# Graph attention in pairs of key tiles: three PSUM score tiles in one exponential, the scores issued in two fours, and the first head loads spread over the projection loop

## The chip, the cores and the metric

The kernel runs on one core of one Trainium2 chip. The metric is the device time of one execution in microseconds (us). A profiled execution gives a span (first to last instruction on the core) and a trace of every instruction. Engine names: PE is TensorE (matmuls), PEld its weight loads, ACT is ScalarE, DVE is VectorE, POOL is GpSimd, and SP is the engine whose queue issues most DMAs.

## The reference, cut to what matters

Four graph layers run one after the other on x (3327 nodes, 128 features) with an adjacency matrix adj of 0 and 1. The change lies in the second, an attention over all nodes with 128 heads of width 8 (n, m run over nodes, d over the 128 heads, h over the 8 elements of a head). Both biases of the score are adj, so 2·adj is added:

```python
q = (x @ Wq.T).reshape(d, n, h)
k = (x @ Wk.T).reshape(d, n, h)
v = (x @ Wv.T).reshape(d, n, h)
a = jnp.einsum('dnh,dmh->dnm', q, k) * scale
a = a + spatial_encoding + edge_encoding      # both are adj
a = jax.nn.softmax(a, axis=2)
out = jnp.einsum('dnm,dmh->dnh', a, v)
```

So there are 128 × 3327 × 3327 scores, and each needs a product, an addition of 2·adj, an exponential, and a weighted sum with v. The sum of the exponentials comes out of the same product as the weighted values, since v carries a ninth column of ones.

## The kernel before

The first layer fills the first 345 us of the profile, the preparation of the attention (projections, L422 to L498) runs to about 566, the attention itself (L500 to L628) from there to 10470, and the two last layers take the rest.

**Preparation.** A loop over 26 row tiles r projects q, k and v. ACT copies each product out of PSUM into a staging tile (`qk_st`, `v_st`; four buffers of each), and SP stores it to DRAM. A fresh `v_st` tile needs its column of ones, which POOL writes with a memset in each round (L473). From r = 2 on, one entry of the list `early` is emitted in each round: `Parting` loads queries and keys back, splits each into a rounded part and a rest, and stores both (L356 to L381); `load_heads(0, 0)` loads the keys, queries and values of the first four heads, 20 DMAs in one entry; `key_pair` rounds two key tiles on POOL (L419); `exp_of` makes exponentials of 2·adj (L347). Outside the hand-ordered part, a scheduler may move instructions of one engine past each other.

**Attention.** Queries are taken in 7 chunks of 476 columns (the last 471, run as 472), heads in 32 groups of four, keys in 26 tiles t of 128. So there are 7 × 32 × 26 = 5824 steps, or 2912 pairs of an even and an odd key tile. The order on every engine is that of the program text (`manual_schedule`, L578). Head i of a group lies on rows 32i to 32i + 31, so four score matmuls can run side by side on four row groups. `WAYS` (L505) says how 2·adj gets into a score: D, DVE adds it while it moves the scores out of PSUM (L552); I, an identity matmul adds it in PSUM (L550); G, POOL multiplies the finished exponential by exp(2·adj) (L555). An even tile is D, D, D, I and an odd one D, D, I, G. D scores go to the PSUM tile `early`, four buffers of one bank. I and G scores go to the tile `late`, one bank for an even tile and two for an odd one, one buffer each. A last bank, `acc`, takes the weighted sums. ACT exponentiates the `late` scores directly (L553, once per step), and the five D scores of a pair in one instruction in SBUF (L557). `weigh` (L559) issues the four value matmuls of the step four steps back; they use four column groups, in two passes each. At the end of a group, DVE copies `acc` out (L573).

On PE, a step is: four scores, identity product or products, weigh. On ACT, a pair is: exponential of 476 columns, of 952, of 2380.

Of the kernel before, what the change touches and what calls it, by code (L numbers as in the profile page):

```python
# [8 lines left out]
F32 = mybir.dt.float32  # L9
# [6 lines left out]
AF = mybir.ActivationFunctionType  # L16
# [5 lines left out]
P = 128  # L22
# [32 lines left out]
def kernel(  # L55
# [285 lines left out]
    def even(c):  # L341
        w = q_chunks[c][1]
        return w + w % 2
# [45 lines left out]
                if t == 11:  # L389
                    self.store(side)  # L390

    def load_heads(c, g):
        q0, w = q_chunks[c]
        k_in = kq.tile([P, NP], F32, name="k_in", bufs=1)
        q4 = kq.tile([P, QW], F32R, name="q4")
        v4 = kq.tile([P, 4, T, EA], F32, name="v4")
        nc.gpsimd.memset(k_in[:, N:], 0.0)
        if w % 2:
            nc.gpsimd.memset(q4[:, w : w + 1].bitcast(F32), 0.0)
        for i in range(4):  # L400
            n0 = (4 * g + i) * N
            for j in range(2):
                r = 32 * i + HL * j
                nc.sync.dma_start(k_in[r : r + HL, :N], kt[:, n0 : n0 + N])
                nc.sync.dma_start(q4[r : r + HL, :w].bitcast(F32), dram(qt, E * j * GP + n0 + q0, [[0, 2], [GP, E], [1, w]]))
        for i in range(4):
            n0 = (4 * g + i) * N
            nc.sync.dma_start(
                v4[:, i].rearrange("p t e -> p (t e)"),
                vd[n0 : n0 + NP, :].rearrange("(p t) e -> p (t e)", t=T),  # L410
            )
        return k_in, q4, v4, []

    def key_pair(heads):
# [7 lines left out]
    with tc.tile_pool(name="l1", bufs=1) as pool, tc.tile_pool(name="l1_ps", bufs=3, space=PSUM) as ps:  # L422
        w_st = pool.tile([D, 3, NH * E], F32, name="w_st")
        for i, w in enumerate((wq, wk, wv)):
            nc.gpsimd.dma_start(w_st[:, i, :], w)
        zero = pool.tile([HL, NH], F32, name="zero")
        nc.vector.memset(zero, 0.0)
        nc.gpsimd.dma_start(vd[N * NH : N * NH + 1, :], zero[:1, :EA])
        for end in (qf, kf):
            nc.gpsimd.dma_start(end[:E, N * NH :], zero[:E])  # L430

        with tc.tile_pool(name="l1_ln", bufs=1) as ln, tc.tile_pool(name="l1_tp", bufs=2, space=PSUM) as tps:
            h, done = layernorm_relu(ln)
            done(T)
            hT = transposed(pool, tps, h, "hT")
        st = ctx_st.enter_context(tc.tile_pool(name="l1_st", bufs=4))

        def store(dst, src, r, kp):
            for p0, p1 in ((0, kp),) if kp == P else ((0, 112), (112, kp)):
                nc.sync.dma_start(dst[r * P + p0 : r * P + p1], src[p0:p1])  # L440


        assert 7 * N + NP <= 2 * P * NH
        early = []
        for g in range(2):
            part = Parting(g)
            for side in range(2):
                early.append(lambda part=part: (part.load(0), part.load(1)) if part.lo[0] is None else None)
                early.append(lambda part=part, side=side: [part.part(side, i) for i in range(4)] and part.store(side))
        first, e_first = [], []  # L450
        early.append(lambda: first.extend(load_heads(0, 0)))
        ahead_part = Parting(2)
        early.append(lambda: (ahead_part.load(0), ahead_part.load(1)))
        early.append(lambda: e_first.extend(exp_of(a, 0) for a in a_first[1::2]))
        early += [lambda: (key_pair(first), key_pair(first))] * (T // 4)
        if T // 2 % 2:
            early.append(lambda: key_pair(first))
        for r in range(T):
            kp = rows_of(r)
            lhs = hT[:, r * P : r * P + kp]  # L460
            for i, (dst, mx) in enumerate(((qf, q_max), (kf, k_max))):
                pp = ps.tile([P, 2, 512], F32, name="pp", bufs=2)
                for c in range(2):
                    nc.tensor.matmul(pp[:kp, c, :], lhs, w_st[:, i, c * 512 : c * 512 + 512], start=True, stop=True)
                s = st.tile([P, E * NH], F32, name="qk_st")
                nc.scalar.activation(s[:kp], pp[:kp].rearrange("p a b -> p (a b)"), AF.Copy, scale=D**-0.5 if i == 0 else 1.0)
                nc.vector.tensor_reduce(mx[:kp, r : r + 1], s[:kp], AX.X, ALU.max, apply_absolute_value=True)
                store(dst[:E].rearrange("e (r c) -> r e c", c=NH), s.rearrange("p (e c) -> p e c", c=NH), r, kp)
            pp = ps.tile([P, 2, 512], F32, name="pp", bufs=2)
            for c in range(2):  # L470
                nc.tensor.matmul(pp[:kp, c, :], lhs, w_st[:, 2, c * 512 : c * 512 + 512], start=True, stop=True)
            s = st.tile([P, NH, EA], F32, name="v_st")
            nc.gpsimd.memset(s[:, :, E : E + 1], 1.0)  # L473
            nc.scalar.copy(s[:kp, :, :E], pp[:kp].rearrange("p a (c e) -> p (a c) e", e=E))
            store(vd.rearrange("(r c) e -> r (c e)", c=NH), s.rearrange("p c e -> p (c e)"), r, kp)

            if r > 1 and early:
                early.pop(0)()
        while early:
            early.pop(0)()  # L480

        mx4 = pool.tile([P, 4], F32, name="mx4")
        for i, m in enumerate((q_max, k_max, a_max, low_bits)):
            nc.vector.tensor_reduce(mx4[:, i : i + 1], m, AX.X, ALU.max)
        all4 = pool.tile([P, 4], F32, name="all4")
        nc.gpsimd.partition_all_reduce(all4, mx4, P, bass_isa.ReduceOp.max)
        bound = pool.tile([P, 1], F32, name="bound")
        nc.vector.tensor_mul(bound, all4[:, 0:1], all4[:, 1:2])  # L490
        nc.vector.tensor_scalar_mul(bound, bound, 1.01 * E / 2)
        nc.vector.tensor_add(bound, bound, all4[:, 2:3])
        fits = pool.tile([P, 2], F32, name="fits")
        nc.vector.tensor_scalar(fits[:, 0:1], bound, SAFE / 2, None, op0=ALU.is_le)
        nc.vector.tensor_scalar(fits[:, 1:2], all4[:, 3:4], 0.0, None, op0=ALU.is_equal)
        nc.vector.tensor_mul(unsafe, fits[:, 0:1], fits[:, 1:2])
        nc.vector.tensor_scalar(unsafe, unsafe, -1.0, 1.0, op0=ALU.mult, op1=ALU.add)
        ctx_st.close()  # L498
# [3 lines left out]

    WAYS = ("DDDI", "DDIG")  # L505
    PLACES = ((0, 1, 2, 5), (3, 4, 6, 7))
    two_i = const.tile([P, P], BF16, name="two_i")
    nc.vector.tensor_copy(two_i, ident)
    engines = {
# [9 lines left out]
    with tc.tile_pool(name="at_in", bufs=1) as a_pool, tc.tile_pool(name="at_p", bufs=3) as p_pool, tc.tile_pool(  # L519
# [13 lines left out]
            q0, w = q_chunks[c]  # L533
            nc.sync.dma_start(adj16[t][:, q0 : q0 + w], a2[:, :w])

        def scores(step, heads, a2, e_a, p8):
            c, _, t = step
            we = even(c)
            _, q4, _, pairs = heads
            ways, places = WAYS[t % 2], PLACES[t % 2]  # L540
            n_d = ways.count("D")
            late = ps.tile([P, 4 - n_d, 512], F32, name=f"late{4 - n_d}")
            early = [ps.tile([P, 512], F32, name="early", bufs=4) for _ in range(n_d)]
            for i in (*range(n_d, 4), *range(n_d)):
                r = slice(32 * i, 32 * i + 32)
                sp = early[i] if i < n_d else late[:, i - n_d]
                nc.tensor.matmul(sp[:, :we], pairs[t // 2][r, t % 2, :], q4[r, :we], start=True, stop=ways[i] != "I")  # L547
            for i in range(4):
                if ways[i] == "I":
                    nc.tensor.matmul(late[:, i - n_d, :we], two_i, a2[:, :we], start=False, stop=True)  # L550
            for i in range(n_d):
                nc.vector.tensor_tensor(p8[:, places[i], :we], early[i][:, :we], a2[:, :we], op=ALU.add)  # L552
            nc.scalar.activation(p8[:, places[n_d] : places[3] + 1, :we], late[:, :, :we], AF.Exp)  # L553
            if ways[3] == "G":
                nc.gpsimd.tensor_tensor(p8[:, places[3], :we], p8[:, places[3], :we], e_a[:, :we], op=ALU.mult)  # L555
            if t % 2:
                nc.scalar.activation(p8[:, :5, :we], p8[:, :5, :we], AF.Exp)  # L557

        def weigh(step, v4, p8):  # L559
            c, g, t = step  # L560
# [17 lines left out]
        with tc.manual_schedule(engines=engines):  # L578
# [7 lines left out]
            for j, step in enumerate(steps):  # L586
# [6 lines left out]
                        a_t, a_next = a_next, []  # L593
                        e_t, e_next = e_next, []
                if t % 2 == 0:
                    p8 = p_pool.tile([P, 8, QW], F32, name="p8")
                scores(step, heads, a_t[t], e_t[t // 2], p8)
                begun[j] = (step, heads[2], p8)
                if j >= ahead:
                    weigh(*begun.pop(j - ahead))  # L600
                if t == min(4, T // 2) and more:
                    coming = load_heads(*groups[n])
                if c == 0 and g + 2 < n_groups:
# [506 lines left out]
```

## Time and profile before

| | |
|---|---|
| median of 3 runs | 11194.51 us (11192.19 to 11195.0) |
| profiled execution, its time | 11195.14 us |
| profiled execution, its span | 11193.4 us |
| TensorE clock granted | 0.989 |
| attention stage in the trace | 566 to 10470 us |
| PE, ACT, DVE, POOL busy over the span | 97, 91, 83, 54% |

In a row of the groups view, the columns are: line, engine, operation, output from input, shapes, count, then busy time and mean ns of one, then the idle time of the engine just before these instructions and what ended it. In the timeline, each row has start, duration, engine, line and a count of merged instructions. An ACT instruction's duration holds the time that it waits behind the one before it, so durations of successive rows overlap; the steps between starts and between ends tell the rate. Durations of PE matmuls are modelled and overlap as well.

### The profile page before, as it was taken

The numbers are of one execution on the slowest core, as the hardware profiler recorded it, in microseconds if no ns is written. First come the engines' busy times: TensorE is split into PE (matmuls) and PEld (weight loads), VectorE is DVE, ScalarE is ACT, GpSimd is POOL, SyncE is SP. The second block draws the span as 40 slices with busy tenths as digits, with TensorE's granted clock in tenths as the row PEclk, the third lists the DMA queues.
The fourth block names the chain that finished last, engine by engine and source line by source line (L and its number), as shares of the span: only waits on it lengthen the run. The fifth ranks groups of instructions, "written<-read, shape, count | busy, mean of one in ns | idle before, by whom it ended". The sixth has DMA issues, their size and how long they took to land. (4 is left out here: it accounts for less than half of the span.)

```text
span 11193.4 us, 209350 instructions
## 1 busy us (share of the span) xinstructions
PE 10850.5 (97%) x79530; PEld 3005.9 (27%) x79530; DVE 9343.1 (83%) x15429; ACT 10199.3 (91%) x9152; POOL 6016.3 (54%) x6964
## 2 busy tenths in 40 slices
PE   9899999999999999999999999999999999999996
PEld 4322222222222222222222222222222222222453
DVE  8588888888888888888888888888888888888656
ACT  0399999999999999999999999999999999999522
POOL 0277777555555555555555555555555555555203
PEclk9899999999999999999999999999999999999998
DMA  7755554333333333333333333333333332333432
GB/s 264 238 129 120 123 127 109 65 64 64 68 64 62 67 66 63 68 65 61 68 66 63 66 66 61 67 66 61 66 66 61 66 63 55 61 58 58 135 113 97
DMA packets 417541, 942.25 MB, mean 84 GB/s; under 512 B 67936, under 2 KB 345937, under 8 KB 380940
## 3 DMA queue, kind: packets, MB, share of 16 engines
q1 hardware_dynamic: 412762, 918.98, 37.4%
q8 instruction: 627, 10.27, 0.4%
q0 software_dynamic: 3760, 9.78, 0.3%
q14 instruction: 392, 3.21, 0.1%
HBM read 788.78 MB, written 139.71 MB: 83 GB/s over the span
## 5 line engine op out<-in xcount | busy, mean ns | idle before, releaser
L552 DVE TENSOR_TENSOR p<-early,a 128x476 f32<-128x476 f32 (+1 forms) x14560 | 8426.4, 646 | 1369.4 <-PE early L547 1297.5
L557 ACT ACTIVATE p<-p 128x2380 f32<-128x2380 f32 (+1 forms) x2912 | 7568.4, 2599 | 0.4
L564 PE MATMUL acc<-p,v 128*9 128x476 f32 (+1 forms) x46592 | 5748.5, 564 | 15.3 <-ACT p L557 1.4
L553 ACT ACTIVATE p<-late 128x476 f32<-128x476 f32 (+1 forms) x5824 | 5315.4, 1175 | 13.8 <-DMA q<-qt 10.2
L555 POOL TENSOR_TENSOR p<-p,e 128x476 f32<-128x476 f32 (+1 forms) x2912 | 3528.1, 1212 | 3204.3 <-ACT p L553 2998.6
L547 PE MATMUL late<-q,k 32*128 32x476 f32 (+1 forms) x8736 | 2798.2, 478 | 99.5 <-ACT p L553 39.7
L547 PE MATMUL early<-q,k 32*128 32x476 f32 (+1 forms) x14560 | 2843.6, 478 | 9.4 <-DVE p L552 9.4
L419 POOL CAST k<-k_in 128x256 fp32r<-128x256 f32 x2912 | 1936.5, 697 | 886.4 <-DMA k_in<-kt 339.4
L547 PEld LDWEIGHTS late<-q,k 32*128 32x128 f32 x8736 | 1065.4, 181 | 4890.4 <-ACT p L553 4186.2
L550 PE MATMUL late<-a,two_i 128*128 128x476 bf16 (+1 forms) x5824 | 2180.8, 374 | 0.0
L547 PEld LDWEIGHTS early<-q,k 32*128 32x128 f32 x14560 | 1113.0, 181 | 9.9 <-DVE p L552 9.9
L564 PEld LDWEIGHTS acc<-p,v 128*9 128x9 f32 x46592 | 695.2, 88 | 1272.6 <-issue 1185.8
L550 PEld LDWEIGHTS <-two_i 128*128 128x128 bf16 x5824 | 556.2, 96 | 1329.0 <-issue 1329.0
L189 ACT COPY agg<-agg_ps 128x512 f32<-128x512 f32 x15 | 8.2, 591 | 485.5 <-PE agg_ps L204 290.6
L230 PE MATMUL agg_ps<-a,part 128*128 128x512 bf16 (+1 forms) x1092 | 227.0, 369 | 4.3 <-ACT agg L928 3.2
L272 POOL TENSOR_SCALAR a<-a_in 128x476 bf16<-128x476 f32 (+2 forms) x156 | 221.1, 1417 | 0.5
L272 POOL TENSOR_SCALAR a<-a 128x476 bf16<-128x476 f32 (+1 forms) x26 | 36.4, 1400 | 288.1 <-DMA a<-in_adjT_dram 288.1
L923 PE MATMUL sp<-yT,hT 128*128 128x512 f32 (+1 forms) x364 | 170.7, 610 | 12.3 <-ACT agg L928 6.4
L204 PE MATMUL agg_ps<-a,h 128*128 128x512 f32 (+2 forms) x364 | 148.2, 570 | 26.2 <-DVE h L164 26.2
L573 DVE COPY o<-acc 105x476 f32<-105x476 f32 (+1 forms) x224 | 144.5, 645 | 4.6 <-PE acc L564 4.6
L204 PE MATMUL agg_ps<-a,x 128*128 128x512 f32 (+2 forms) x364 | 145.3, 562 | 0.6 <-ACT x L318 0.6
L230 PEld LDWEIGHTS <-part 128*128 128x128 f16 x1092 | 108.6, 99 | 117.7 <-issue 10.3
(236 smaller groups left out, 2592.0 us busy)
## 6 DMA issues: line engine op xcount, KB each, us to landing
k_in<-kt SPq DMA_DIRECT2D x1792, 207.9 KB
v<-vd SPq DMA_DIRECT2D x896, 117.0 KB
a<-in_adjT_dram SPq DMA_DIRECT2D x50, 1663.5 KB
a<-adj SPq DMA_DIRECT2D x78, 831.8 KB
q<-qt SPq DMA_DIRECT2D x1536, 29.8 KB
a_in<-in_adjT_dram SPq DMA_DIRECT2D x125, 238.0 KB
adj<-a SPq DMA_DIRECT2D x156, 119.0 KB
vd<-v_st SPq DMA_DIRECT2D x25, 576.0 KB
```

The lines of the kernel that those rows point to most:

```text
L204: nc.tensor.matmul(acc[c][:, :w], lhs[:kp, t, :], a[:kp, c0 : c0 + w], start=(t == 0), stop=(t == T - 1))
L230: nc.tensor.matmul(acc[c][:, :w], part[:, t, :], a[:, c0 : c0 + w], start=(t == 0 and i == 0), stop=(t == T - 1 and i == len(parts) - 1),)
L272: nc.gpsimd.tensor_scalar(a2[:kp, :w], a, 2.0, None, op0=ALU.mult)
L419: nc.gpsimd.tensor_copy(k, slots(k_in)[:, t : t + 2, :])
L547: nc.tensor.matmul(sp[:, :we], pairs[t // 2][r, t % 2, :], q4[r, :we], start=True, stop=ways[i] != "I")
L550: nc.tensor.matmul(late[:, i - n_d, :we], two_i, a2[:, :we], start=False, stop=True)
L552: nc.vector.tensor_tensor(p8[:, places[i], :we], early[i][:, :we], a2[:, :we], op=ALU.add)
L553: nc.scalar.activation(p8[:, places[n_d] : places[3] + 1, :we], late[:, :, :we], AF.Exp)
L555: nc.gpsimd.tensor_tensor(p8[:, places[3], :we], p8[:, places[3], :we], e_a[:, :we], op=ALU.mult)
L557: nc.scalar.activation(p8[:, :5, :we], p8[:, :5, :we], AF.Exp)
L564: nc.tensor.matmul(acc[32 * i : 32 * i + EA, :w], v4[:kp, i, t, :], p8[:kp, PLACES[t % 2][i], :w], start=(t == 0), stop=(t == T - 1),)
L923: nc.tensor.matmul(sp[:, c0 : c0 + w], slots(zT)[:, t, :], z2T[:, cols], start=True, stop=False)
```

## The change

Four edits are made together.

1. `WAYS` of an even tile becomes I, D, D, D. `scores` is called once for a pair. The three `late` scores of a pair (the even tile's I, the odd tile's I and G) share one tile of three banks, in one buffer, and one exponential of 3 × 476 columns. `early` keeps its four banks, so all eight banks are in use as before.
2. The eight scores of a pair are issued as two fours, each on four row groups. The first four are all D (even heads 1, 2, 3 and odd head 0). The second are the three late ones and the fifth D (odd head 1). Between the two fours goes the weigh of the even tile; after the second come both identity products, one behind the other, and then the weigh of the odd tile.
3. POOL's multiplication is issued at the odd step (`times_e`), behind what POOL is given in the even step.
4. In the preparation, `load_heads(0, 0)` is cut in pieces: four entries with four key and query DMAs each, then one value DMA in each of the next four entries. Each of seven entries rounds two key tiles and makes two exponentials (the last entry has one of each). Two empty entries of `early` go. The four `v_st` tiles are made once, with the column of ones written before the loop.

The diff, cut to its core:

```diff
-    def load_heads(c, g):
+    def load_heads(c, g, pieces=None):
...
+        for f in (scored, weighted):
+            for i in range(4):
+                if pieces is None:
+                    f(i)
+                else:
+                    pieces.append(lambda f=f, i=i: f(i))
...
-        first, e_first = [], []
-        early.append(lambda: first.extend(load_heads(0, 0)))
         ahead_part = Parting(2)
         early.append(lambda: (ahead_part.load(0), ahead_part.load(1)))
-        early.append(lambda: e_first.extend(exp_of(a, 0) for a in a_first[1::2]))
-        early += [lambda: (key_pair(first), key_pair(first))] * (T // 4)
-        if T // 2 % 2:
-            early.append(lambda: key_pair(first))
+        pieces, e_first = [], []
+        first = load_heads(0, 0, pieces)
+        early += pieces[:4]
+        key_steps = -(-(T // 2) // 2)
+        for i in range(key_steps):
+            def step(i=i):
+                for f in pieces[4 + i : 5 + i if i < key_steps - 1 else None]:
+                    f()
+                for n in (2 * i, 2 * i + 1):
+                    if n < T // 2:
+                        key_pair(first)
+                        e_first.append(exp_of(a_first[2 * n + 1], 0))
+            early.append(step)
+        v_sts = [st.tile([P, NH, EA], F32, name=f"v_st{i}", bufs=1) for i in range(4)]
+        for s in v_sts:
+            nc.gpsimd.memset(s[:, :, E : E + 1], 1.0)
...
-            s = st.tile([P, NH, EA], F32, name="v_st")
-            nc.gpsimd.memset(s[:, :, E : E + 1], 1.0)
+            s = v_sts[r % 4]
...
-    WAYS = ("DDDI", "DDIG")
-    PLACES = ((0, 1, 2, 5), (3, 4, 6, 7))
+    WAYS = ("IDDD", "DDIG")
+    PLACES = ((5, 0, 1, 2), (3, 4, 6, 7))
+    FOURS = (((0, 1), (0, 2), (0, 3), (1, 0)), ((0, 0), (1, 2), (1, 3), (1, 1)))
...
+            p8 = p_pool.tile([P, 8, QW], F32, name="p8")
+            late = ps.tile([P, 3, 512], F32, name="late")
+            for n, four in enumerate(FOURS):
+                if n == 1:
+                    between()
+                for odd, i in four:
+                    way, place = WAYS[odd][i], PLACES[odd][i]
+                    sp = ps.tile([P, 512], F32, name="early", bufs=4) if way == "D" else late[:, place - 5]
+                    r = slice(32 * i, 32 * i + 32)
+                    nc.tensor.matmul(sp[:, :we], pairs[t // 2][r, odd, :], q4[r, :we], start=True, stop=way != "I")
+                    if way == "D":
+                        nc.vector.tensor_tensor(p8[:, place, :we], sp[:, :we], a2s[odd][:, :we], op=ALU.add)
+            for odd, i in FOURS[1]:
+                if WAYS[odd][i] == "I":
+                    nc.tensor.matmul(late[:, PLACES[odd][i] - 5, :we], two_i, a2s[odd][:, :we], start=False, stop=True)
+            nc.scalar.activation(p8[:, 5:, :we], late[:, :, :we], AF.Exp)
+            nc.scalar.activation(p8[:, :5, :we], p8[:, :5, :we], AF.Exp)
+            return p8
...
                 if t % 2 == 0:
-                    p8 = p_pool.tile([P, 8, QW], F32, name="p8")
-                scores(step, heads, a_t[t], e_t[t // 2], p8)
+                    p8 = scores(step, heads, a_t[t : t + 2], lambda: weigh(*begun.pop(j - ahead)) if j >= ahead else None)
+                else:
+                    times_e(step, p8, e_t[t // 2])
+                    if j >= ahead:
+                        weigh(*begun.pop(j - ahead))
                 begun[j] = (step, heads[2], p8)
-                if j >= ahead:
-                    weigh(*begun.pop(j - ahead))
```

More of the change, by code (lines that the diff above doesn't have):

```diff
@@ L399, in load_heads, with scored @@
             nc.gpsimd.memset(q4[:, w : w + 1].bitcast(F32), 0.0)
-        for i in range(4):
+        def scored(i):
             n0 = (4 * g + i) * N
@@ L405, in load_heads, with weighted @@
                 nc.sync.dma_start(q4[r : r + HL, :w].bitcast(F32), dram(qt, E * j * GP + n0 + q0, [[0, 2], [GP, E], [1, w]]))
-        for i in range(4):
+        def weighted(i):
             n0 = (4 * g + i) * N
@@ L447 @@
             for side in range(2):
-                early.append(lambda part=part: (part.load(0), part.load(1)) if part.lo[0] is None else None)
+                if side == 0:
+                    early.append(lambda part=part: (part.load(0), part.load(1)))
                 early.append(lambda part=part, side=side: [part.part(side, i) for i in range(4)] and part.store(side))
-        first, e_first = [], []
-        early.append(lambda: first.extend(load_heads(0, 0)))
         ahead_part = Parting(2)
         early.append(lambda: (ahead_part.load(0), ahead_part.load(1)))
-        early.append(lambda: e_first.extend(exp_of(a, 0) for a in a_first[1::2]))
-        early += [lambda: (key_pair(first), key_pair(first))] * (T // 4)
-        if T // 2 % 2:
-            early.append(lambda: key_pair(first))
+        pieces, e_first = [], []
[14 more added lines that the diff above has]
+            nc.gpsimd.memset(s[:, :, E : E + 1], 1.0)
         for r in range(T):
@@ L534, in store_adj, with scores @@
             nc.sync.dma_start(adj16[t][:, q0 : q0 + w], a2[:, :w])
-        def scores(step, heads, a2, e_a, p8):
+        def scores(step, heads, a2s, between):
             c, _, t = step
@@ L539, in scores @@
             _, q4, _, pairs = heads
[L540 to L555, printed above, removed]
@@ L556, in scores @@
-            if t % 2:
-                nc.scalar.activation(p8[:, :5, :we], p8[:, :5, :we], AF.Exp)
+            p8 = p_pool.tile([P, 8, QW], F32, name="p8")
[10 more added lines that the diff above has]
+                        nc.vector.tensor_tensor(p8[:, place, :we], sp[:, :we], a2s[odd][:, :we], op=ALU.add)
@@ new lines, in scores, with times_e @@
+            for odd, i in FOURS[1]:
[4 more added lines that the diff above has]
+            return p8
+        def times_e(step, p8, e_a):
+            we = even(step[0])
+            assert WAYS[1][3] == "G"
+            nc.gpsimd.tensor_tensor(p8[:, PLACES[1][3], :we], p8[:, PLACES[1][3], :we], e_a[:, :we], op=ALU.mult)
```

## The prediction

> **What bounds the kernel now.** I read the engine totals, then the busy time by stretches, then waits and timelines inside one stretch.
>
> ```profile
> PE 10850.5 (97%) x79530; PEld 3005.9 (27%) x79530; DVE 9343.1 (83%) x15429; ACT 10199.3 (91%) x9152; POOL 6016.3 (54%) x6964
> ...
> L552 DVE TENSOR_TENSOR p<-early,a 128x476 f32<-128x476 f32 (+1 forms) x14560 | 8426.4, 646 | 1369.4 <-PE early L547 1297.5
> L557 ACT ACTIVATE p<-p 128x2380 f32<-128x2380 f32 (+1 forms) x2912 | 7568.4, 2599 | 0.4
> ...
> L553 ACT ACTIVATE p<-late 128x476 f32<-128x476 f32 (+1 forms) x5824 | 5315.4, 1175 | 13.8 <-DMA q<-qt 10.2
> ```
>
> Over the whole span PE looks like the bound. But both rows of exponentials have almost no idle time before them, and 91% is an average: outside the attention ACT does little. In one thousand us of the attention (columns: length, then busy us of PE, PEld, DVE, ACT, POOL):
>
> ```profile
> 5000.00:6000.00 1000.00, 992.29 (x7678) 243.96 (x7678) 865.87 (x1499) 1000.00 (x888) 561.26 (x627) 1.00 0.35 66
> ```
>
> ACT has no gap at all. The waits say who follows whom, PE's weight load behind ACT:
>
> ```profile
> PEld late L547 <- ACT p L553: 4186.2, 4941, 1.6
> ```
>
> The timelines of ACT, PE and DVE over one pair of key tiles:
>
> ```profile
> 5035.00 2.69 ACT L557 ACTIVATE p<-p 128x2380 f32<-128x2380 f32 x1
> 5037.09 1.90 ACT L553 ACTIVATE p<-late 128x476 f32<-128x476 f32 x2
> 5038.39 2.69 ACT L557 ACTIVATE p<-p 128x2380 f32<-128x2380 f32 x1
> ```
>
> ```profile
> 5036.45 0.48 PE L547 MATMUL late<-q,k 32*128 32x476 f32 x2
> 5036.46 0.48 PE L547 MATMUL early<-q,k 32*128 32x476 f32 x2
> 5036.88 0.38 PE L550 MATMUL late<-a,two_i 128*128 128x476 bf16 x1
> 5037.18 0.99 PE L564 MATMUL acc<-p,v 128*9 128x476 f32 x8
> 5038.19 0.47 PE L547 MATMUL late<-q,k 32*128 32x476 f32 x1
> 5038.20 0.49 PE L547 MATMUL early<-q,k 32*128 32x476 f32 x3
> ```
>
> ```profile
> 5038.84 2.90 DVE L552 TENSOR_TENSOR p<-early,a 128x476 f32<-128x476 f32 x5 [0.48 <-PE early L547]
> ```
>
> A pair takes 3.388 us: even fours start at 5000.93 and, 70 pairs later, at 5238.06. On PE a four gives way to the identity product after 0.423, that to the weigh after 0.310, that to the next four after 0.910 where nothing is waited for (means over these pairs). That is 1.643 per step and 3.286 per pair; at each even step PE waits the last 0.1, and starts 0.05 after the 476-column exponential ends (5037.09 + 1.05 = 5038.14, then 5038.19). DVE starts 0.64 after the four and takes 2.90 for five additions, so it idles 0.48 to 0.49. **ACT is the bound by 0.1 us a pair, with PE right behind.** 2912 pairs at 3.388 are 9866 of the 9904 us of the stage.
>
> **What the Trainium skill says.** *TensorEngine Tiling (Array Packing)*, Key Properties: changing the tiling mode drains TensorE. The trace agrees: each first load of an identity or value product sits idle 0.21 to 0.23 us with nothing awaited. *TensorE: Matmul & The Clock Gate*, Part 2, says that a weight load is pulled ahead of a running matmul when row groups differ or when it goes to the background buffer. The trace agrees for full-array bf16 products: 28 of those at L230 (24 of 512 columns, 4 of 255), each with a load of its own, follow one another in 5.62 us (10619.72 to 10625.34), which leaves nothing for the loads. *ScalarE: Activation LUTs*, Specifications, gives 1.2 GHz, 0.833 ns per element; L928 agrees, 1967 ns at 2048 columns against 1324 at 1279, 0.836 ns each.
>
> **ACT's part.** End to end, the three exponentials of a pair cost 0.45, 0.86 and 2.08 us. At 0.833 ns, 476 columns are 0.397, so about 0.05 to 0.06 per instruction is left over. One instruction of 1428 columns is then 1.19 + 0.055 = 1.245 in place of 1.31. ACT's pair falls to **3.325**. A straight line through the three costs gives 0.03 per instruction and 3.36; if all that lies between the first two were saved, 3.32. I take 3.33, ends 3.32 and 3.36. If nothing else bound, that would be 0.058 × 2912 = 169 us.
>
> **PE's part.** The fours, the eight value matmuls per step and the two identity products per pair stay. One change of mode goes. The new pair is four to weigh 0.423 (not in the trace; a four before an identity product is the nearest, and I allow 0.40 to 0.47), weigh to four 0.910, four to identity 0.423, identity to identity 0.20 (476 columns at the L230 rate), identity to weigh 0.310, weigh to four 0.910: **3.176**. Were the second load of the identity not hidden (0.096 us, 556.2 us for 5824 at L550), it would be 3.27. Either is under ACT's 3.33, so it looks as if the whole of ACT's gain arrives.
>
> **The wait that is added.** It sits in the `early` banks. A pair takes five of them in turn out of four, so the fourth score of a first four, (1, 0), needs the bank that the fifth addition of the pair before has just read. Today a pair takes them as three and two, with an identity product and a weigh in between, and no such wait shows. Call Y the time at which PE comes to a first four, and Z that at which its fourth score goes. The first three need banks that are free by then, so DVE starts at Y + 0.64, has five additions done at Y + 3.54, and the next (1, 0) can go 0.05 later (the weigh starts 0.05 after DVE's copy of `acc` at L573, 5052.56 to 5052.61). Behind a waiting (1, 0) stands all of PE: even weigh, second four, identity products, odd weigh, and then the next first four, at Z + 3.176. So from the Z of one pair to the Z two pairs on, 3.176 + 0.64 + 2.90 + 0.05 = 6.766 us pass, **3.383 per pair**. PE waits 0.21 per pair on DVE, and DVE still idles 0.48, for it waits on the three scores that PE brings late. ACT gets 0.05 of idle time per pair.
>
> **Group ends.** In one pair of 13, DVE also copies `acc`. Now this hides in ACT's surplus. Then the copy follows the odd weigh (at Z + 2.27, so Y + 2.48; ended at 3.47, DVE starting 0.11 later as now, 0.64 of copy), ends about 4.22 after Y, and delays the next even weigh (otherwise at Y + 4.02) by 0.26 and the next addition by 0.12. In the loop above that is some 0.18 per group, 0.014 per pair. The attention then has 3.397 per pair against 3.388: 0.009 × 2912 = **26 us more**.
>
> **Other edits, at no cost.** POOL's multiplication has two pairs (6.8 us) from its exponential to its weigh, for 1.21 us of work. The identity products and the odd weigh move behind the second four; late scores of the next pair need the merged exponential, which ends some 0.9 before PE comes there. These covers are gone only if a pair falls under 3.33.
>
> **The preparation.** SP issues the same 20 head DMAs (16 for keys and queries, 4 for values), four per round and then one, in place of 20 at once. Now they hold SP's queue from 471 to 491 and the projections' stores behind it; ACT then waits:
>
> ```profile
> 496.17 1.02 ACT L466 ACTIVATE qk_st<-pp 128x1024 f32<-128x1024 f32 x1 [18.07 <-DMA qf<-qk_st]
> ```
>
> ```profile
> 400.00:500.00 100.00, 67.97 (x132) 28.10 (x131) 27.20 (x23) 33.47 (x33) 24.23 (x48) 0.83 0.83 243
> 500.00:560.00 60.00, 59.27 (x135) 25.89 (x134) 26.49 (x22) 33.84 (x34) 4.51 (x13) 0.97 1.02 315
> ```
>
> The column before the last is the DMA share. It is full from 500 on, so only the holes before that can be won: 17 us. POOL's memsets fall from 26 to 4 and with them 102.5 us of its waiting for `vd` stores, behind which splitting and rounding are queued; thirteen exponentials of 0.5 us fit in ACT's gaps of 0.7. I take **15 us less**, between 30 less and 5 more, as the new DMAs also stand ahead of stores.
>
> **Sum.** 11195.14 (the profiled execution, 0.6 above the median) + 26 − 15 = **11206 us**, +0.1%. No change means within 0.2%, 22 us, about what a measurement of this kernel can tell. This case's own range is 11150 to 11270: 0.02 us in a pair is 58 us.
>
> **The rivals.**
> (1) *ACT stays the bound.* The loop through the four banks is shorter than my sum by 0.1 (the two intervals that no trace shows, or DVE's start). It then lies at 3.33 per pair: 11195 − 169 − 15 = 11011, up to 11100 if only part is won. For it: PE's own 3.176 and DVE's 2.82 between starts leave room; against: every term but two is measured. Chance 0.2.
> (2) *PE pays for the identity pair*: the second load of the identity is not pulled ahead behind a product on the same rows, 0.096 us. The loop is 6.862, 3.431 and 3.445 with group ends: 0.057 × 2912 − 15 = +151, 11346. It decides as soon as the two-pair loop exceeds 6.77. L230 speaks against it; for it, that PE then stood in one mode for long, and here enters it for two products. Chance 0.3, with any other lengthening of that loop of the same size.
> (3) *The merged exponential doesn't save an instruction's cost*, because what is left over belongs to each row of 476: ACT 3.36. The banks still decide, and the time is that of the forecast.
>
> **How the numbers follow.** Forecast, with (3), 0.5: a fifth of it falls below −0.2%, two fifths within, two fifths above. (1) is almost wholly faster, (2) wholly slower. Faster 0.1 + 0.2 = 0.30, same 0.21, slower 0.49. The range leaves out the better half of (1) and the worse third of (2): 11050 to 11340.
>
> **What would show it.** Right: PE waiting at early scores on DVE, near 600 us in total, where the page now has 9.4; the wait of late scores on ACT gone; ACT idle some 0.05 per pair; even-weigh starts 0.42 after a first four. Wrong: ACT still without a gap at 3.33 (rival 1); identity products 0.3 apart (rival 2); a merged exponential above 1.28 from end to end (rival 3).

## The result and the profile after

| | before | after |
|---|---|---|
| median (12 runs each) | 11194.25 us (11188.99 to 11197.49) | 11200.22 us (11196.81 to 11203.63) |
| profiled execution: time, span | 11195.14, 11193.4 us | 11196.81, 11195.0 us |
| first to last exponential of late scores | 576.2 to 10469.7, 9893.5 us | 569.5 to 10476.6, 9907.1 us |
| what follows the last one | 723.7 us | 718.4 us |

The ratio after to before is 1.0005, 95% interval 0.9997 to 1.0014: no difference that can be told. The forecast was 11206.

In the page of the kernel after, the groups that belong to the attention read (line, engine, operation, output from input, shapes, count, then busy us and mean ns, then the idle time just before and what ended it):

```profile
PE 10881.3 (97%) x79530; PEld 3009.4 (27%) x79530; DVE 9348.0 (84%) x15429; ACT 10146.0 (91%) x6240; POOL 6019.0 (54%) x6942
...
L577 DVE TENSOR_TENSOR p<-early,a 128x476 f32<-128x476 f32 (+1 forms) x14560 | 8413.4, 644 | 1339.7 <-PE early L575 1285.3
L582 ACT ACTIVATE p<-p 128x2380 f32<-128x2380 f32 (+1 forms) x2912 | 6366.0, 2186 | 0.0
...
L581 ACT ACTIVATE p<-late 128x1428 f32<-128x1428 f32 (+1 forms) x2912 | 3961.3, 1360 | 82.5 <-PE late L580 63.9
```

The totals of the engines are as before to within 0.6% (the largest change is ACT's, 10199.3 to 10146.0); on their own they tell nothing. The row of the long exponential does: its mean fell from 2599 to 2186 ns, with the same 2380 columns. An ACT duration holds the time behind the instruction ahead, so the long exponential now waits less behind the one ahead of it. The row of the merged exponential has idle time before it that its predecessors had not. Busy time in the same thousand us of the attention (length, then PE, PEld, DVE, ACT, POOL, granted clock, DMA share, GB/s) agrees, with ACT at 993 where it was 1000:

```profile
5000.00:6000.00 1000.00, 991.37 (x7658) 243.40 (x7656) 864.82 (x1496) 993.03 (x590) 559.54 (x624) 1.00 0.35 66
```

Now the timeline of PE after, over two pairs and into the end of a group of 13 (start, duration, engine, line, tiles, shape, count):

```profile
5038.48 0.85 PE L575 MATMUL early<-q,k 32*128 32x476 f32 x4
5039.26 0.98 PE L595 MATMUL acc<-p,v 128*9 128x476 f32 x8
...
5040.60 0.58 PE L580 MATMUL late<-a,two_i 128*128 128x476 bf16 x2
5041.11 0.99 PE L595 MATMUL acc<-p,v 128*9 128x476 f32 x8
5042.02 0.49 PE L575 MATMUL early<-q,k 32*128 32x476 f32 x4
5042.44 0.99 PE L595 MATMUL acc<-p,v 128*9 128x476 f32 x8
...
5045.20 0.86 PE L575 MATMUL early<-q,k 32*128 32x476 f32 x4
...
5047.83 0.99 PE L595 MATMUL acc<-p,v 127*9 127x476 f32 x8
5048.75 0.49 PE L575 MATMUL early<-q,k 32*128 32x476 f32 x4
5049.62 0.69 PE L595 MATMUL acc<-p,v 128*9 128x476 f32 x4 [0.38 <-DVE o L604]
```

and of DVE:

```profile
5039.08 2.89 DVE L577 TENSOR_TENSOR p<-early,a 128x476 f32<-128x476 f32 x5 [0.29 <-PE early L575]
5042.64 2.89 DVE L577 TENSOR_TENSOR p<-early,a 128x476 f32<-128x476 f32 x5 [0.66 <-PE early L575]
5045.81 2.89 DVE L577 TENSOR_TENSOR p<-early,a 128x476 f32<-128x476 f32 x5 [0.28 <-PE early L575]
5048.91 0.65 DVE L604 COPY o<-acc 105x476 f32<-105x476 f32 x1 [0.21 <-PE acc L595]
```

The first fours (x4, all `early`) last 0.85, 0.49 and 0.86. A four that waits for nothing takes 0.49; the other 0.37 is the fourth score, which waits for a bank. The fourth of 5045.20 goes when DVE's additions of the pair before are done: 5042.64 + 2.89 = 5045.53. From waiting four to waiting four two pairs pass, in 6.72 us; between them lie 3.54 and 3.18. At 5048.75 the group ends: the weigh that elsewhere follows a first four after 0.42 follows after 0.87, behind DVE's copy of `acc` (5048.91 + 0.65 = 5049.56).

**Theory** for the experiments: ACT was the bound before. Merging made it faster than the loop through the four `early` banks, which now sets the pair. One turn of this loop spans two pairs: PE works from a fourth score that waited to the next first four (PE's leg, 3.18), DVE starts behind that four (0.61), makes five additions (2.89), and frees the bank for the next fourth score that waits (0.05): 6.73 in all. And the end of a group, which ACT used to cover, is paid in full. **Rivals**: ACT remains the bound; or PE's own order of fours and products is what takes the time, whatever the banks do.

### The profile page after: what moved, and what is told of

It is laid out like the page before. It is cut to its first block, busy times and chain, and to the rows that moved or that the text cites. A ratio compares the mean times of both kernels' runs of the same rounds, so it can differ in the third digit from the quotient of the medians.

```text
span 11195.0 us, 206613 instructions
## 1 busy us (share of the span) xinstructions
PE 10881.3 (97%) x79530; PEld 3009.4 (27%) x79530; DVE 9348.0 (84%) x15429; ACT 10146.0 (91%) x6240; POOL 6019.0 (54%) x6942
## 5 line engine op out<-in xcount | busy, mean ns | idle before, releaser
L582 ACT ACTIVATE p<-p 128x2380 f32<-128x2380 f32 (+1 forms) x2912 | 6366.0, 2186 | 0.0
L581 ACT ACTIVATE p<-late 128x1428 f32<-128x1428 f32 (+1 forms) x2912 | 3961.3, 1360 | 82.5 <-PE late L580 63.9
L575 PE MATMUL early<-q,k 32*128 32x476 f32 (+1 forms) x14560 | 3314.7, 478 | 10.2 <-DVE p L577 9.1
L429 POOL CAST k<-k_in 128x256 fp32r<-128x256 f32 x2912 | 1942.3, 699 | 912.0 <-DMA k_in<-kt 381.5
L575 PEld LDWEIGHTS early<-q,k 32*128 32x128 f32 x14560 | 1337.1, 181 | 2576.5 <-DVE p L577 2566.3
L580 PE MATMUL late<-a,two_i 128*128 128x476 bf16 (+1 forms) x5824 | 1675.4, 369 | 0.0
L575 PE MATMUL late<-q,k 32*128 32x476 f32 (+1 forms) x8736 | 1414.6, 478 | 34.7 <-ACT p L581 34.4
L575 PEld LDWEIGHTS late<-q,k 32*128 32x128 f32 x8736 | 547.4, 181 | 2357.9 <-ACT p L581 1188.0
L580 PEld LDWEIGHTS <-two_i 128*128 128x128 bf16 x5824 | 331.1, 97 | 664.0 <-issue 664.0
L272 POOL TENSOR_SCALAR a<-a_in 128x476 bf16<-128x476 f32 (+2 forms) x156 | 221.8, 1422 | 0.5
L272 POOL TENSOR_SCALAR a<-a 128x476 bf16<-128x476 f32 (+1 forms) x26 | 36.4, 1402 | 287.0 <-DMA a<-in_adjT_dram 287.0
```

The costliest lines, as they stand in the source:

```text
L272: nc.gpsimd.tensor_scalar(a2[:kp, :w], a, 2.0, None, op0=ALU.mult)
L429: nc.gpsimd.tensor_copy(k, slots(k_in)[:, t : t + 2, :])
L575: nc.tensor.matmul(sp[:, :we], pairs[t // 2][r, odd, :], q4[r, :we], start=True, stop=way != "I")
L580: nc.tensor.matmul(late[:, PLACES[odd][i] - 5, :we], two_i, a2s[odd][:, :we], start=False, stop=True)
L581: nc.scalar.activation(p8[:, 5:, :we], late[:, :, :we], AF.Exp)
```

## The experiments

Eight kernels ran in two groups, on two chips, each group with its own runs of the kernel before (medians 11188.83 and 11188.84). "More" and "less" below are against these runs; the kernel after itself was not run again with them. Where no ratio is given, the kernel ran once. A pair's time below is from starts in the trace; a group's is the step from one copy of `acc` to the next. The kernel before has 44.04 us per group, the kernel after 44.16 (13 × 3.397 of the forecast is 44.16 too).

**The two halves of the change.** The kernel before with the new preparation only:

```diff
-    def load_heads(c, g):
+    def load_heads(c, g, pieces=None):
...
+        first = load_heads(0, 0, pieces)
+        early += pieces[:4]
...
+            s = v_sts[r % 4]
```

> The kernel before with the change's preparation alone (head loads in pieces, four lasting v_st tiles, exponentials beside the key rounding). Theory (two parts that nearly cancel): the first attention exponential starts 6 to 8 us earlier than the 576.2 of before and the attention itself keeps its length, so 5 to 10 us less than before. Rival (the preparation is bound by DMA and only moved, and the earlier start comes from elsewhere): first exponential at 576, no change.

Measured: 11181.42 (12 runs), ratio 0.9994, interval 0.9985 to 1.0002. That is 7.4 us less, which this measurement doesn't separate from none. In the trace the first late exponential starts at 567.3 in place of 576.2. And the kernel after with the old preparation:

```diff
-    def load_heads(c, g, pieces=None):
+    def load_heads(c, g):
...
-            s = v_sts[r % 4]
+            s = st.tile([P, NH, EA], F32, name="v_st")
+            nc.gpsimd.memset(s[:, :, E : E + 1], 1.0)
```

> The changed kernel with the old preparation. Theory: first exponential at 575 to 577, attention from first to last late exponential 9907 as in the changed kernel, 13 more than before, so 10 to 18 us more than before, about 0.1%. Rival (the attention change is neutral and the preparation lost time): equal to the kernel before.

Measured: 11208.41 (19 runs), ratio 1.0018, interval 1.0011 to 1.0025, so 19.6 us more, just over the expected end. The first late exponential starts at 576.4, and from there to the last one pass 9914.7 us, 7.6 more than in the trace of the kernel after, where the same was expected: two traces of the same attention differ by that much. So the zero of the whole is a small loss in the attention, which is clear of the noise, and a smaller gain ahead of it, which shows in the traces alone.

**Was ACT the bound before?** The even tile's exponential of 476 columns is left out of the kernel before (the even weigh then takes head 2's exponentials for head 3 too; one part in eight of the weighted sums is not the reference's):

```diff
-            nc.scalar.activation(p8[:, places[n_d] : places[3] + 1, :we], late[:, :, :we], AF.Exp)
+            if t % 2:
+                nc.scalar.activation(p8[:, places[n_d] : places[3] + 1, :we], late[:, :, :we], AF.Exp)
...
-                    p8[:kp, PLACES[t % 2][i], :w],
+                    p8[:kp, PLACES[t % 2][i] if t % 2 else min(PLACES[0][i], 2), :w],
```

> The kernel before, with the 476-column exponential of every even tile left out (the weigh of that head reads the place of head 2 instead). Theory (ACT bound the kernel before, PE close behind): ACT falls to 2.94 per pair, PE's own 3.286 shows, with 0.2 to 0.3 per group end: 3.29 to 3.31 per pair, 230 to 290 us less, 10900 to 10965. Rival (PE bound the kernel before, as its 97% say): no change, 11190.

Measured: 10954.23. The same thousand us as above:

```profile
5000.00:6000.00 1000.00, 997.12 (x7846) 246.37 (x7839) 883.83 (x1533) 948.88 (x604) 574.72 (x645) 1.00 0.35 67
```

ACT has 51 us of gaps and PE has next to none. A group takes 43.09, 3.315 per pair with the group's end in it. So ACT was the bound, and PE came 0.07 behind (3.388 against 3.315).

**Is it the merging that pays?** The exponential of the kernel after is cut in two again, all else kept:

```diff
-            nc.scalar.activation(p8[:, 5:, :we], late[:, :, :we], AF.Exp)
+            nc.scalar.activation(p8[:, 5:6, :we], late[:, 0:1, :we], AF.Exp)
+            nc.scalar.activation(p8[:, 6:, :we], late[:, 1:, :we], AF.Exp)
```

> The merged exponential of three late banks is cut again into 476 and 952 columns; all else is the changed kernel. Theory (the four early banks set the pace: PE's leg of 3.18, DVE's start and five additions, in 6.73 us per two pairs): ACT goes back to 3.388 us per pair, which is just under the 3.397 that a pair takes with group ends, so 11200 to 11240. Rival (ACT is still the bound, its saving arrives and is lost elsewhere): 0.055 x 2912 = 160 us more, 11360.

Measured: 11210.73 (16 runs), ratio 1.0020, interval 1.0012 to 1.0028.

```profile
5000.00:6000.00 1000.00, 992.17 (x7656) 244.41 (x7656) 864.45 (x1495) 999.51 (x885) 562.45 (x626) 1.00 0.35 65
```

ACT is at 999.5 of 1000, and yet two pairs take 6.73 as in the kernel after, and a group 44.19, where ACT's own 13 × 3.388 are 44.04. Two bounds lie 0.3% apart, and an ACT row without gaps does not say which of them it is. The 5824 exponentials that became 2912 were worth about 0.0015 of the time (1.0020 against 1.0005, each to before on its own chip), some 16 us, in place of the 169 that ACT alone would have won. The two profiled executions differ by 13.6, and their traces say where: the ordinary groups are 0.023 longer in the mean, 5 us over 217 of them, and the six in which ACT also makes the next chunk's exponentials of 2·adj take 49.8 in place of 48.7, 6 us; the start and the end of the stage make up the rest.

**Does the bank loop set the pair?** The fifth addition reads a constant in SBUF in place of its bank, so the fourth score of the next first four waits for no addition any more, and the third only for the fourth addition (one score of eight is left out of the result):

```diff
-                        nc.vector.tensor_tensor(p8[:, place, :we], sp[:, :we], a2s[odd][:, :we], op=ALU.add)
+                        seen = ones.to_broadcast([P, we]) if (odd, i) == (1, 1) else sp[:, :we]
+                        nc.vector.tensor_tensor(p8[:, place, :we], seen, a2s[odd][:, :we], op=ALU.add)
```

> The fifth addition of a pair (odd head 1) reads ones from SBUF in place of its score bank, so that bank is free as soon as it is written; DVE keeps five additions, PE all its products, ACT both exponentials. Left out: the scores of that head in odd key tiles. Theory (the bank that the fourth score waits for): PE's waits for DVE at early scores go, the pair falls to ACT's 3.33 or 3.35 with group ends, 11005 to 11065. Rival A (DVE's own additions set the pace): no change, 11200. Rival B (PE's changes of mode set it): no change, 11200.

Measured: 11121.7. That is 67 us less, so the bank counts, but it misses my range by more than 50. The trace shows why. PE's wait at the first fours is gone (0.005 in the mean, group ends apart). But this kernel's additions, all at one line, fall into two rows:

```profile
L578 DVE TENSOR_TENSOR p<-early,a 128x476 f32<-128x476 f32 x9984 | 5819.1, 644 | 681.4 <-PE early L575 642.6 <-ACT p L582 8.1 <-DMA vd<-v_st 7.3
L578 DVE TENSOR_TENSOR p<-ones,a 128x476 f32<-128x476 f32 x2496 | 2094.5, 839 | 0.0
```

The addition from SBUF takes 839 ns in the mean against 644 from PSUM. In its timeline, DVE, POOL and PE:

```profile
5016.77 1.50 DVE L578 TENSOR_TENSOR p<-ones,a 128x476 f32<-128x476 f32 x1
```

```profile
5016.55 1.21 POOL L589 TENSOR_TENSOR p<-p,e 128x476 f32<-128x476 f32 x1
```

```profile
5018.40 0.48 PE L575 MATMUL late<-q,k 32*128 32x476 f32 x3
5018.89 0.47 PE L575 MATMUL early<-q,k 32*128 32x476 f32 x1
```

DVE's addition ends 0.51 after POOL's multiplication (5018.27 against 5017.76): it looks held until POOL is through. The next additions start late, and PE now waits 0.49 in the second four, for the bank of its single D score. The Trainium skill, *SBUF — State Buffer*, "Who interferes with whom", says that a DVE instruction with two SBUF inputs contends with a GpSimd instruction that reads SBUF, because its second input comes through a read interface that the two engines share. Over this whole trace the addition takes 1.49 in the median where it starts beside POOL's multiplication (649 cases), 0.85 beside POOL's cast at L429 (486), and 0.64 with POOL free (1535). Beside the one-input TENSOR_SCALAR at L272, which reads SBUF as well, it also takes 0.64 (147), so the rule is not seen for that one. The edit that was to remove a wait brought another: this experiment shows that the bank counts, and leaves open by how much.

**Is PE's order the bound?** One of the two identity products is left out (one score of eight lacks its 2·adj):

```diff
-                    nc.tensor.matmul(sp[:, :we], pairs[t // 2][r, odd, :], q4[r, :we], start=True, stop=way != "I")
+                    nc.tensor.matmul(sp[:, :we], pairs[t // 2][r, odd, :], q4[r, :we], start=True, stop=way != "I" or not odd)
...
-                if WAYS[odd][i] == "I":
+                if WAYS[odd][i] == "I" and odd:
```

> The identity product of the even tile is left out (its 2 adj is not added to head 0 of even key tiles), so PE's leg from one fourth score to the next first four is 0.20 shorter, 2.98; DVE and ACT are as in the changed kernel. Theory (the bank loop is PE's leg plus DVE's chain): two pairs need 6.53, under ACT's 6.66, so ACT binds at 3.33 to 3.35, 11000 to 11070. Rival A (DVE's additions set the pace): 11200. Rival B (PE alone sets it): 0.20 x 2912 = 580 less, 10620.

Measured: 11005.5. The total alone doesn't refute that rival, since ACT's 3.326 would have stopped it too. The starts of the first fours do. Behind a group end, before ACT comes up, two pairs take 6.54:

```profile
5009.28 0.62 PE L575 MATMUL early<-q,k 32*128 32x476 f32 x4
5015.82 0.65 PE L575 MATMUL early<-q,k 32*128 32x476 f32 x4
```

That is 0.19 less than 6.73, one identity product (0.20) less in two pairs; PE's order alone would have lost it in each pair. And both fours wait, for 0.13 and 0.16 (0.62 and 0.65 in place of 0.49). Then ACT becomes the bound: the tile view of the late exponential in this kernel (duration min/median/max in ns, then first and last start) is

```profile
L581 ACT ACTIVATE p<-late x2912: 1351/2002/2324, 570.7 to 10281.8; 128x1428 f32<-128x1428 f32 x167, 128x1416 f32<-128x1416 f32 x28
```

A median of 2002, against 1361 in the kernel after, means that these exponentials queue. A group takes 43.24, 3.326 per pair. This is ACT's floor after merging. From the end of the long exponential to its own end the merged one takes 1.25 here, where its two predecessors took 0.46 and 0.86. Both figures answer the rival by which the saving would belong to rows and not to instructions (3.36, and an exponential above 1.28).

**The group ends.** The copy of `acc` reads a constant in SBUF, so that no weigh waits for it (the weighted sums are left out of the result):

```diff
-                nc.vector.tensor_copy(o4[: 96 + EA, :w], acc[: 96 + EA, :w])
+                nc.vector.tensor_copy(o4[: 96 + EA, :w], ones[: 96 + EA].to_broadcast([96 + EA, w]))
```

> DVE's copy at the end of a group reads ones from SBUF in place of the accumulator, so the next weigh does not wait for it and the copy does not wait for the last weigh; DVE still runs one copy per group. Left out: the weighted sums. Theory: a group falls from 44.16 us to 13 x 3.366 = 43.76, up to 43.9 as DVE's copy still takes its slot; 0.26 to 0.40 x 224 = 58 to 90 us less, 11110 to 11142. Rival (group ends are hidden and the steady loop alone accounts for the time): no change, 11200.

Measured: 11126.68, 62 us less. A group takes 43.82 in place of 44.16, so the copy with its wait is worth 0.34 in each, 76 over 224 groups. (The copy itself is also shorter, 0.40 against 0.65; the two aren't told apart here.)

**A shorter loop with everything computed.** Even heads 1 and 2 go to two neighbouring banks, and one DVE instruction of 2 × 476 adds both; head 3 goes ahead of them, and the three single D scores share the two other banks:

```diff
-    FOURS = (((0, 1), (0, 2), (0, 3), (1, 0)), ((0, 0), (1, 2), (1, 3), (1, 1)))
+    FOURS = (((0, 3), (0, 1), (0, 2), (1, 0)), ((0, 0), (1, 2), (1, 3), (1, 1)))
...
+                    if (odd, i) == (0, 2):
+                        a_two = a2s[0][:, :we].unsqueeze(1).to_broadcast([P, 2, we])
+                        nc.vector.tensor_tensor(p8[:, 0:2, :we], two[:, :, :we], a_two, op=ALU.add)
```

> DVE adds even heads 1 and 2 in one instruction of 2 x 476 columns out of two neighbouring banks (2 adj read twice by a broadcast), with even head 3 added first and the two single banks taken in turn; five additions become four instructions. The order of the fours is otherwise that of the changed kernel, and all is computed. Theory (bank loop): the chain of additions is one start shorter, 0.07, so two pairs need 6.66 and a pair 3.33, beside ACT's 3.326; with group ends of 0.36 per 13 pairs 3.35 to 3.36, so 0.035 to 0.045 x 2912 = 100 to 130 us less than the changed kernel and below the kernel before: 11065 to 11100. Rival (PE's changes of mode or ACT's work set the pace): no change, 11200. Rival (the longer first release makes PE wait elsewhere, as the double addition frees two banks late): 11200 to 11300.

Measured: 11120.19 (5 runs), ratio 0.9939, interval 0.9925 to 0.9953. This beats both kernels. The timeline of DVE over one pair:

```profile
5042.99 0.65 DVE L587 TENSOR_TENSOR p<-early,a 128x476 f32<-128x476 f32 x1 [0.66 <-PE early L582]
5043.56 1.14 DVE L585 TENSOR_TENSOR p<-two,a 128x952 f32<-128x952 f32 x1
5044.62 1.20 DVE L587 TENSOR_TENSOR p<-early,a 128x476 f32<-128x476 f32 x2
```

A pair's additions take 2.83 in place of 2.89, and two pairs 6.67 (PE's first fours at 5042.38 and 5049.05): 0.06 taken out of DVE is 0.06 out of the loop, close to ACT's floor of 2 × 3.326 = 6.652. A group takes 43.78, which leaves 0.42 for its end with pairs of 3.335. It missed my range by 20 us, by the group ends, which I had still counted too low.

## Why the prediction was right

The forecast was 6 us from the median, and its main point holds: the gain on ACT is lost to a wait for an `early` bank. Part of the closeness is luck: two terms were off by some 50 us each, with opposite signs. Nor was the forecast sure of itself: it gave no change a chance of 0.21 and a slower kernel 0.49. In the order of its steps:

- **ACT's part**, 3.325 (3.33 taken): right, 3.326 where ACT is saturated. So an instruction less is 0.06 us. The upper end of 3.36 came from a sum that doesn't come out: a straight line through 0.45, 0.86 and 2.08 leaves 0.044 per instruction, not 0.03, so 3.34.
- **PE's part**, 3.176: right, 5045.20 − 5042.02 = 3.18. Four to weigh was bounded by 0.40 to 0.47 and is 0.42. The identity products to the weigh take 5041.11 − 5040.60 = 0.51, as 0.20 + 0.31. So the second load of the identity doesn't show, even where PE enters the mode for two products only. This fits what the Trainium skill says of a load to the background buffer (*TensorE: Matmul & The Clock Gate*, Part 2); to which buffer it went, the trace doesn't tell. Rival (2) falls.
- **The wait that is added**: right in kind and place. Shown by the waiting fours and, from the other side, by the kernel with one double addition. The loop is 6.73 and not 6.766: the term that was off is DVE's start behind PE, 0.61 in place of 0.64. That is 3.366 per pair, 0.017 × 2912 = 50 us too much in the forecast.
- **PE's wait**: 0.21 per pair foretold, 0.18 measured, and not even: 0.37 in one pair and 0.01 in the next. The measure is the time from a first four to its weigh, less 0.42: 482 us in all, without the one pair in each group whose weigh waits for the copy of `acc`, and another 102 us in those. The forecast wanted to see near 600 us in the row of early scores. No such number is in the views. That row still has 9.1 us of idle, since the first three scores of the four are running; the weight loads' row has far more:

```profile
PEld early L575 <- DVE p L577: 2566.3, 4180, 9.5
```

  Most of this lies beside running matmuls. The forecast named a wrong view for a right wait. Two other signs came in part. ACT's gaps are 7 us in the thousand, 0.02 per pair in place of 0.05. And the wait of late scores on ACT is still in the views, though smaller:

```profile
PEld late L575 <- ACT p L581: 1188.0, 1443, 1.4
```

  This too is idle time of weight loads: from a weigh to the next four PE takes 0.916 in the median and 0.918 or less in nine cases of ten, as it does where nothing is waited for.
- **Group ends**: the step that was off most. 0.18 per group was foretold; 44.157 − 13 × 3.366 = 0.40 is measured. The addition behind the copy is late by 0.12, as worked out. The weigh is late by 0.45, not 0.26: in 185 of the 224 groups the pair that makes the copy wait is one that waited over 0.3 itself (at 5045.20 it was 0.37), so its odd weigh, 2.63 after that pair's first four and not 2.48, and the copy come later. The forecast put the average wait where the long one belongs. 0.22 × 224 = 49 us too little.
- **The attention's sum**: 26 us were foretold, as pairs that hardly change and cheap ends. It is −0.022 × 2912 = −64 for the pairs and 0.40 × 224 = +90 for the ends. Whole stage in the trace: +13.6. Most of the rest has a name. In six groups ACT also makes the next chunk's 13 exponentials of 2·adj; such a group took 50.3 us before and takes 48.7 now, since part of this fits in ACT's new gaps. That is −10 us, and it was missing in the forecast. The 2 us left over are less than what one trace can fix, as the 7.6 between two traces of the same attention show.
- **The preparation**: 15 less foretold, 6.7 measured here (569.50 against 576.21). Other kernels of this study with the new preparation start between 567.3 and 570.9. The holes were filled in part: the DMA share from 400 to 500 us rose to 0.90 and not to 1.

```profile
400.00:500.00 100.00, 74.14 (x150) 30.00 (x148) 29.28 (x24) 36.81 (x37) 14.72 (x27) 0.91 0.90 268
```

  The forecast saw one stall of 18.07 us go. It is now four of 3 to 4, one in each round with head DMAs, as in this row of ACT:

```profile
492.40 1.02 ACT L490 ACTIVATE qk_st<-pp 128x1024 f32<-128x1024 f32 x1 [3.84 <-DMA qf<-qk_st]
```

- **After the attention**, which the change doesn't touch, 5.3 us less: other kernels have 718 to 722 there. Without it, the profiled execution would be 11202 and not 11197.

From the forecast to the profiled execution these terms add up: 11206 − 50 (pairs) + 49 (group ends) − 10 (six groups) − 2 (left over) + 8 (preparation) − 5 (after the attention) = 11196, where 11197 was measured.

Rivals (1) and (3) are refuted by ACT's gaps together with pairs of 3.366, and by ACT's floor of 3.326. What remains open is what the bank's wait alone is worth, since the kernel that was to take it away brought a wait of its own, and why the time after the attention moves by some us from kernel to kernel.

## What to carry to other kernels

Where one engine is saturated and another is 2 to 3% behind, as PE was here, instructions saved on the first alone are worth that gap at most, and less if the rearrangement that saves them closes a loop through few buffers. So count for each pool how many instructions later a buffer is needed again, and add up the loop once around, over as many iterations as it spans. Work at the end of a loop that was free under the old bound has to be priced anew, with the long wait of an uneven loop and not its mean. When the result is a loop of buffers, shorten the engine inside it (here one instruction for two banks, 0.6%) rather than the one that was the bound before.

## What the runs showed of the hardware

- One addition over two neighbouring PSUM banks, 2 × 476 columns, takes 1.06 us from its start to that of the next instruction (5043.56 to 5044.62); two single ones take 1.13, (2.89 − 0.64) / 4 × 2.
- An addition of 476 columns with both inputs in SBUF takes 0.64 us alone, as from PSUM, 0.85 beside a POOL cast, and about 1.5 us beside a POOL multiplication that reads SBUF, ending 0.51 after it. It was not delayed beside POOL's one-input TENSOR_SCALAR (0.64).
- Two identity products of 476 columns in a row, each with its own weight load, take 0.51 us to the next mode, and one took 0.31: the second adds 0.20, and its load doesn't show.
- One exponential of 1428 columns out of PSUM takes 1.25 us from end to end on a saturated ACT, one of 476 and one of 952 take 0.46 and 0.86: an instruction less saves 0.06.
- DVE's first addition starts 0.61 us after the four that it reads from; PE goes on 0.05 after DVE's last addition frees the bank.
